# Leaving chunk steps out of table slots, and a block-diagonal product on quarters of the array

## The chip, the cores and the metric

The kernel runs on one NeuronCore of a Trainium2 chip. The metric is the time of one execution on the device, in microseconds (us); lower is better. All tensors are fp32.

## The reference, cut to what matters

The model has two layers. Layer 0 is a deformable attention block on `x` of shape (2, 512, 32, 32), followed by an output projection and an MLP with residuals; layer 1 is a plain attention over the 1024 positions with 512 channels. What matters here is the attention of layer 0:

```python
off = tanh(einsum(gelu(depthwise_6x6_stride4(q)), off_pw_w)) * 4      # per group: 64 key positions
kv  = grid_sample(xn, grid + off)                                      # (b, 512, 8, 8)
k   = gconv1x1(kv, kw);  v = gconv1x1(kv, vw)                          # 8 groups of 64 channels
pos  = grid_q[:, :, None, :] - grid_kv[:, None, :, :]                  # 1024 queries x 64 keys
bias = sign(pos) * log1p(abs(pos))
bias = relu(bias @ cpb_w1 + cpb_b1)                                    # 2 -> 128
bias = relu(bias @ cpb_w2 + cpb_b2)                                    # 128 -> 128
bias = bias @ cpb_w3 + cpb_b3                                          # 128 -> 1
attn = softmax(q k^T * scale + bias);  out = attn @ v
x    = x + einsum(out, out_w) + out_b
```

The bias network is evaluated for 16 (batch, group) pairs x 1024 queries x 64 keys, so its 128x128 layer is most of the arithmetic. The value weights `vw` are 8 separate 64x64 blocks; the kernel multiplies them into `out_w` once, so that the sampled features can be multiplied by the product directly.

## The kernel before

**Slots.** The bias network is worked through in 256 slots (`for s in range(NS)`), 16 for each pair of batch and group; a slot covers all queries for 4 keys. TensorE (PE) does 32 matmuls of layer 2 in a slot (`st_layer2`, L633): four groups `z`, each a PSUM tile of 128x1024 that four 32-column tiles of the array fill, in two instructions for each fp32 matmul. The profile therefore counts 64 records a slot. Before that, VectorE (DVE) writes layer 1's output `h1` (`st_layer1`, L616) two slots ahead of its use, in one of three buffers. After each group `z`, ScalarE (ACT) evicts it from PSUM with the ReLU (L642 into `rx`, L644 into `ua`, `uo`, `uc` or `ub`), and DVE sums pairs of evicted tiles (`st_sum`, L652). DMAs that add, issued by GpSimd (POOL) at L654 and L671 and by SyncE (SP) at L678 and L687, fold the sums further; `st_layer3` (L719, with the products of queries and keys at L702) takes the rest every eighth slot.

**PSUM.** The pool `zp` has three buffers of 128x1024. The four groups of a slot go through them in turn, and every other product in the slots (`flat(...)`) takes the next buffer of the same three.

**Table slots.** Each fourth slot (`s % 4 == 0`) also makes the layer-1 tables of the next four slots: a load on SP (`load_tables`, L585) and two ACT instructions (`st_tables`, L596 and L604), queued behind the eviction of group 1.

**Tails.** Softmax over finished logits (`softmax_steps`) is cut into steps too. A step runs in slots that are not table slots, behind the eviction of group 1 (in the last 16 slots in table slots too, there behind group 3). The exponentials (L757) of two pairs take eight steps, in slots 9, 10, 11, 13, 14, 15, 17 and 18 of each 32.

**Chunk steps.** What prepares the keys runs beside the slots, as a generator `bg = later()` of which one step is taken in a slot, behind the eviction of group 3:

```python
            st_sum(s, 0)
            if bg is not None:
                with tc.issue_after(evicted[s][1]):
                    next(bg, None)
```

`later()` first multiplies value weights and output weights (two steps, in slots 0 and 1, L503 and L507, into `uo`), then takes five chains of groups (`CHAINS`). A chain step computes queries (L267, L273, L279), the depthwise convolution (taps on ACT at L319, reductions on DVE at L334), Gelu (L343), the small product (L355), Tanh (L365), key positions (DVE L378 to L389), Abs and Ln on ACT (L392 to L396) and the correction on DVE (L398 to L405), whose result goes out by a DMA on SP to be read by `load_tables`. Its sampling steps (`sample`) prepare hat functions (L421 to L435, L449 to L458), multiply them on DVE (L463), gather with 16 small products (L471), scale and add (ACT L474, DVE L478), and multiply by key weights (L485) and by `uo` (L487), evicted at L491 and L493. They load their inputs on SP (L181, L184, L442, L444). In the profile the last chunk step's products stand in slot 154.

When all chains are through, the slot is noted as `ready`; 4 to 32 slots later DVE prepares blocks for the output projection in eight portions (`spread`, `fold`).

`wv` holds the value weights as four blocks of 128x128, each with two 64x64 blocks on its diagonal and zeros beside them. `QUADS` lists the four quarters of the array: `f_` is the half of the rows (contraction), `h_` the half of the output partitions.

Of the kernel before, what the change touches and what calls it, by code (L numbers as in the profile page):

```python
# [14 lines left out]
P = 128  # L15
B, C, H, W = 2, 512, 32, 32
HW = H * W
NCH = C // P
# [28 lines left out]
def conv_seq_kernel(ctx: ExitStack, tc: tile.TileContext, x, xt, kst, pst, cst, vec, wsm, outw, w1, w2, wl, wlt, brow, out):  # L47
    nc = tc.nc


    QUADS = [(slice(64 * f, 64 * f + 64), slice(64 * h, 64 * h + 64), f, h) for f in range(2) for h in range(2)]
# [50 lines left out]
    def fold(engine, w, sign=ALU.add, which=range(4)):  # L102
        for i in which:
            o, u, v = FOLD[i]
            engine.tensor_tensor(w[o], w[u], w[v], ALU.add if i % 2 else sign)
# [20 lines left out]
    def op_blocks(b, parts, wsum):  # L126
        v, q = vp[:, b * NCH : b * NCH + NCH, :], qa[:, b]
        w = [v[:, k : k + 2, n : n + 256] for k, n in ((0, 0), (2, 0), (2, 256), (0, 256))]
        x = [q[:, k : k + 2, n : n + 512] for k in (0, 2) for n in (0, 512)]
        return w + [wsum[:, j] for j in range(3)], x + [parts[:, j] for j in range(3)]  # L130
# [4 lines left out]
    def flat(name):  # L135
        return zp.tile([P, 2, 512], F32, tag="ps2", name=name).rearrange("p h n -> p (h n)")
# [4 lines left out]
    with tc.tile_pool(name="lp", bufs=2) as lp:  # L141
# [23 lines left out]
        wv = sx.rearrange("p a f j -> p (a f j)")[:, 0:512]  # L165
        ow_s = vp[:, 0:NCH, :]
# [26 lines left out]
        uo = vp[:, NCH : 2 * NCH, :]  # L193
# [302 lines left out]

        def later():

            for k2 in range(2):
                ps = flat("psu")  # L500
                for k in range(2):
                    c = 2 * k2 + k
                    nc.tensor.matmul(  # L503
                        ps[:, 512 * k : 512 * k + 512], wv[:, c * P : (c + 1) * P], ow_s[:, c, :],
                        start=True, stop=True,
                    )
                nc.scalar.copy(uo[:, 2 * k2 : 2 * k2 + 2, :].rearrange("p k o -> p (k o)"), ps)  # L507
                yield
            yield from sample(0)
            for ci in range(1, len(CHAINS)):  # L510
                yield from chain(ci)
                yield from sample(ci)
# [67 lines left out]
        def load_tables(c):  # L580
            b, k, f = groups[c // 4]
            ci, kk = chain_of[b, k]
            assert ci in state
            fb = lp.tile([P, 2, W, KT], F32, name="fb", bufs=1)
            nc.sync.dma_start(  # L585
                out=fb.rearrange("p a x j -> p (a x j)"),
                in_=fdr[ci][f * len(CHAINS[ci]) + kk, c % 4].rearrange("p j -> (p j)").partition_broadcast(P),
            )
            raw[c] = fb
# [18 lines left out]
        def st_layer1(s):  # L608
            ta, tb = tabs[4 * s // KT]
            j = 4 * s % KT  # L610
            h1 = lp.tile([P, H, 4, W], F32, name="h1", bufs=3)
            a = ta[:, j : j + 4, :].rearrange("p t x -> p (t x)")
            b = tb[:, j // 4].rearrange("p y t -> p (y t)")
            step = H // 2 if s == 0 else H
            for y in range(0, H, step):
                nc.vector._custom_dve(  # L616
                    TENSOR_ADD_SAT,
                    out=h1[:, y : y + step].rearrange("p y t x -> p (y t x)"),
                    in0=a.unsqueeze(1).to_broadcast([P, step, 4 * W]),
                    in1=b[:, 4 * y : 4 * (y + step)].unsqueeze(2).to_broadcast([P, 4 * step, W]),  # L620
                    s0=FMAX, s1=0.0,
                )
            h1s[s] = h1


        def st_layer2(s):
            h1 = h1s.pop(s)
            r = []
            for z in range(4):
                ps = zp.tile([P, 2, 512], F32, name="ps2")  # L630
                for h in range(2):
                    for q in range(4):
                        nc.tensor.matmul(  # L633
                            ps[32 * q : 32 * q + 32, h, :], cw2[:, 32 * z : 32 * z + 32],
                            h1[:, 16 * h : 16 * h + 16, q, :], start=True, stop=True,
                        )
                name, bufs = (
                    ("rx", 3), (("ua", 4), ("uo", 2), ("uc", 2), ("uo", 2))[s % 4], ("rx", 3), ("ub", 3)
                )[z]
                o = lp.tile([P, 2, 512], F32, name=name, bufs=bufs)  # L640
                if z % 2 == 0:
                    nc.scalar.activation(o, ps, AF.Relu, bias=sc[:, 4 + z : 5 + z])  # L642
                else:
                    nc.scalar.activation(o, ps, AF.Relu, bias=sc[:, 4 + z : 5 + z], scale=sc[:, z : z + 1])  # L644
                r.append(o)
                if z % 2 == 1:
                    evicted.setdefault(s, []).append(nc.cur_bb.bb.instructions[-1])
            sums[s] = r

        def st_sum(s, z):  # L650
            r = [t.rearrange("p h n -> p (h n)") for t in sums[s][z : z + 2]]
            nc.vector.scalar_tensor_tensor(r[1], r[0], sc[:, z : z + 1], r[1], ALU.mult, ALU.add)  # L652
            if z == 2 and s < NS - 1:
                nc.gpsimd.dma_start(out=sums[s][1], in_=sums[s][3], accum_op=ALU.add)  # L654
                added[0] = nc.cur_bb.bb.instructions[-1]
# [18 lines left out]
        def st_fold(s):  # L674
            add(lanes(s, 0), lanes(s, 1))

        def st_join(s):
            nc.sync.dma_start(out=lanes(s, 1), in_=lanes(s + 1, 1))  # L678
            add(lanes(s, 1), lanes(s + 1, 0))

        def st_fold2(s):
            for o, i in zip(twos(s, 0), twos(s, 1)):
                add(o, i)

        def st_join2(s):
            for o, i in zip(twos(s, 1), twos(s + 2, 1)):
                nc.sync.dma_start(out=o, in_=i)  # L687
            for o, i in zip(twos(s, 1), twos(s + 2, 0)):
                add(o, i)
# [91 lines left out]

        tails = []
        bg = later()
        load_tables(0)
        st_tables(0)
        st_layer1(0)
        st_layer1(1)
        for s in range(NS):
            if s > 0:
                st_sum(s - 1, 2)  # L790
            if s % 2 == 0 and 2 <= s < NS - 2:
                st_fold(s - 2)
            if s % 2 == 1 and 3 <= s < NS - 1:
                st_join(s - 3)
            if s % 4 == 0 and s >= 4:
                st_fold2(s - 4)
            if s % 4 == 2 and s >= 6:
                st_join2(s - 6)
            if s % 4 == 0 and s // 4 + 1 < 4 * NG:
                load_tables(s // 4 + 1)  # L800
            if s + 2 < NS:
                st_layer1(s + 2)
            st_layer2(s)


            if s % 4 == 0 and s // 4 + 1 < 4 * NG:
                with tc.issue_after(evicted[s][0]):
                    st_tables(s // 4 + 1)
            st_sum(s, 0)
            if bg is not None:  # L810
                with tc.issue_after(evicted[s][1]):
                    next(bg, None)
            if bg is not None and state.get(len(CHAINS) - 1, 0) is None:

                bg = None
                php.__exit__(None, None, None)
                opp = tc.tile_pool(name="op", bufs=1, side="right")
                op = opp.__enter__()
                op0 = op_blocks(
                    0, op.tile([P, 3, 2, 512], F32, name="op0x"), op.tile([P, 3, 2, 256], F32, name="op0w")  # L820
                )
                opt = op.tile([P, 2, 512], F32, name="opt")
                ready = s
            if bg is None and s > ready and (s - ready) % 4 == 0 and (s - ready) // 4 <= 8:
                i = (s - ready) // 4 - 1
                if i < 4:
                    spread(op0[1], (i,))
                else:
                    fold(nc.vector, op0[0], which=(i - 4,))
            if tails and (s % 4 or s >= NS - NSL):  # L830
                with tc.issue_after(evicted[s][s % 4 == 0]):
                    if next(tails[0], 0) is not None:
                        tails.pop(0)
            if s % 8 == 4 and s >= 12:
                st_layer3(s - 12)
                if s % NSL == 4:
                    tails.append(softmax_steps(s // NSL - 1))
# [37 lines left out]
    with ExitStack() as top, tc.tile_pool(name="wp", bufs=2) as wp:  # L875
# [171 lines left out]
        for i, (b, p) in enumerate(units):  # L1047

            j, k = divmod(i, NCH)
# [323 lines left out]
```

## Time and profile before

| | |
|---|---|
| median of 3 runs | 2662.8 us (2661.68 to 2663.64) |
| the profiled execution's own time | 2661.0 us |
| its span | 2659.2 us |
| granted TensorE clock | 1.00 |
| PE busy | 2633.2 us (99%) |
| DVE busy | 2241.3 us (84%) |
| ACT busy | 1687.2 us (63%) |
| slots, from 37.2 us on | 1867.3 us for 256 |

A page of the profile gives the busy time of each engine; matmuls overlap, so a busy PE can still hide gaps. A group is named by line, engine, operation and tiles (out<-in), with count, busy time, mean duration in ns of one, and the idle time of its engine just before it with what ended that (the releaser). A timeline line has start, duration, engine, line, operation and, in brackets, the idle time before it. PEld is the load of weights into the array, a row of its own. A window's line has its stretch and length, then each engine's busy time with the number of its instructions, the granted clock, the share of the DMA engines and GB/s.

### The profile page before, as it was taken

The page shows a single profiled execution, that of the slowest core. Times are in us where ns is not written, and L with a number is a line of the kernel's source. Part 1 is how long each engine was busy: PE and PEld are TensorE (multiplying, and loading weights), DVE is VectorE, ACT ScalarE, POOL GpSimd, SP SyncE. Part 2 cuts the span into 40 slices and gives each one's busy share as a digit, 9 for nine tenths or more (in the row PEclk, how much of TensorE's full clock was granted, in tenths as well). Part 3 has the DMA queues.
Part 4 walks back from the last instruction along what each step waited for, and adds up shares of the span by engine and source line. Part 5 has one row for each costly group of instructions (what it writes and reads, how often), then busy time and mean ns, then how long its engine had stood idle before and what let it go on. Part 6 is the DMA issues. An engine that isn't in the chain of part 4 may idle for free.

```text
span 2659.2 us, 46896 instructions
## 1 busy us (share of the span) xinstructions
PE 2633.2 (99%) x19344; PEld 965.0 (36%) x19344; DVE 2241.3 (84%) x1329; ACT 1687.2 (63%) x2201; POOL 792.3 (30%) x867
## 2 busy tenths in 40 slices
PE   9999999999999999999999999999999999999999
PEld 3332322433333333233323323333334444446454
DVE  7999999999999999999999999999674483466354
ACT  5887898789978888877777777777621131114041
POOL 1333333333333333333333333333343232000000
PEclk9999999999999999999999999999999999999999
DMA  5887878888788887888888888878730111000000
GB/s 187 181 176 169 191 164 171 181 189 180 171 176 174 192 175 172 171 177 176 171 172 183 175 178 178 172 173 181 191 110 33 48 48 48 0 16 0 32 0 32
DMA packets 116293, 366.77 MB, mean 138 GB/s; under 512 B 23376, under 2 KB 27616, under 8 KB 113392
## 3 DMA queue, kind: packets, MB, share of 16 engines
q0 software_dynamic: 69408, 235.31, 46.9%
q1 hardware_dynamic: 46240, 128.15, 13.8%
q8 instruction: 153, 2.51, 0.4%
q14 instruction: 60, 0.49, 0.1%
q10 hardware_dynamic: 432, 0.31, 0.0%
HBM read 74.81 MB, written 6.55 MB: 31 GB/s over the span
## 4 chain that ended last, share of the span: by engine, by line
PE 60%; DMA 25%; DVE 7%; issue 6%; ACT 1%; POOL 1%; SPq 0%; POOLq 0%; DVEq 0%; ACTq 0%
PE ps L633 31%; PE sw L956 14%; PE sw L1087 9%; DMA uc<-uo 7%; DMA uc<-uc 6%; DMA ua<-uc 4%; DMA uc<-ub 4%; DVE h L616 3%; PE sw L1185 2%; DMA ua<-uo 1%; DVE ub L652 1%; PE psg L535 1%; DMA ua<-ua 1%; PE sim L719 1%; DVE uo L652 1%
## 5 line engine op out<-in xcount | busy, mean ns | idle before, releaser
L633 PE MATMUL ps<-h,cw 128*32 128x512 f32 x16384 | 1782.8, 592 | 8.1 <-ACT rx L642 6.1
L616 DVE CUSTOM_DVE_ANT_1 h<-ta,tb 128x4096 f32<-128x4096 f32 (+1 forms) x257 | 1131.0, 4402 | 28.1 <-PE ps L633 24.2
L633 PEld LDWEIGHTS ps<-h,cw 128*32 128x32 f32 x16384 | 554.7, 110 | 1205.0 <-issue 1114.6
L642 ACT ACTIVATE rx<-ps,sc 128x1024 f32<-128x1024 f32 x512 | 568.1, 1110 | 146.3 <-PE ps L633 116.4
L644 ACT ACTIVATE ub<-ps,sc 128x1024 f32<-128x1024 f32 x256 | 308.2, 1204 | 80.5 <-PE ps L633 80.2
L652 DVE SCALAR_TENSOR_TENSOR ub<-rx,sc,ub 128x1024 f32<-128x1024 f32 x256 | 326.8, 1277 | 6.6 <-ACT ub L644 6.6
L671 POOL DMA_DIRECT2D ua<-uc x126 | 158.3, 1272 | 299.5 <-DMA ua<-uc 292.5
L671 POOL DMA_DIRECT2D ua<-ua x189 | 225.4, 1336 | 20.2 <-DMA ua<-uo 16.2
L644 ACT ACTIVATE uo<-ps,sc 128x1024 f32<-128x1024 f32 x128 | 154.2, 1205 | 74.3 <-PE ps L633 46.2
L956 PE MATMUL sw<-xb,w1t 128*128 128x512 f32 x448 | 193.7, 592 | 2.7 <-DVE xs L123 2.7
L956 PE MATMUL sw<-hm,w2t 128*128 128x512 f32 x448 | 193.6, 592 | 0.0
L654 POOL DMA_DIRECT2D uo<-ub x127 | 126.8, 998 | 210.8 <-DVE ub L652 200.1
L652 DVE SCALAR_TENSOR_TENSOR uo<-rx,sc,uo 128x1024 f32<-128x1024 f32 x128 | 163.5, 1278 | 18.9 <-ACT uo L644 18.9
L123 DVE TENSOR_TENSOR hm<-hm,sw 128x1024 f32<-128x1024 f32 x56 | 67.6, 1218 | 104.5 <-PE sw L956 104.3
L671 POOL DMA_DIRECT2D uc<-uo x63 | 54.0, 857 | 340.8 <-DMA uc<-uo 340.4
L956 PEld LDWEIGHTS sw<-xb,w1t 128*128 128x128 f32 x448 | 85.0, 190 | 110.2 <-issue 105.7
L965 ACT ACTIVATE hm<-hm,vs 128x512 f32<-128x512 f32 x64 | 42.6, 713 | 128.4 <-DVE hm L123 128.4
L956 PEld LDWEIGHTS sw<-hm,w2t 128*128 128x128 f32 x448 | 85.1, 190 | 107.1 <-issue 106.2
L123 DVE TENSOR_TENSOR xs<-xs,sw 128x1024 f32<-128x1024 f32 (+1 forms) x48 | 55.6, 1171 | 75.9 <-PE sw L1087 36.0
L654 POOL DMA_DIRECT2D ua<-ub x64 | 59.3, 926 | 178.4 <-DVE ub L652 163.4
L1087 PE MATMUL sw<-aT,vt 128*128 128x512 f32 x224 | 96.7, 593 | 0.3 <-ACT aT L1167 0.3
L596 ACT ACTIVATE ta<-fb,vs 128x512 f32<-128x512 f32 (+1 forms) x65 | 88.5, 1364 | 10.1 <-DMA fb<-fdr 10.1
(247 smaller groups left out, 2191.6 us busy)
## 6 DMA issues: line engine op xcount, KB each, us to landing
uo<-ub POOLq DMA_DIRECT2D x127, 512.0 KB, 5.5
fb<-fdr SPq DMA_DIRECT2D x64, 512.0 KB, 5.2
ua<-ub POOLq DMA_DIRECT2D x64, 512.0 KB, 6.0
uc<-ub POOLq DMA_DIRECT2D x64, 512.0 KB, 5.0
ua<-ua POOLq DMA_DIRECT2D x63, 256.0 KB, 6.3
ua<-uo SPq DMA_DIRECT2D x63, 256.0 KB, 2.5
ua<-uo POOLq DMA_DIRECT2D x63, 256.0 KB, 5.6
uc<-uc POOLq DMA_DIRECT2D x63, 256.0 KB, 7.2
```

What stands on the lines that cost most here:

```text
L123: nc.vector.tensor_tensor(out, a, b_, op)
L596: nc.scalar.activation(ta.rearrange("p j x -> p x j")[:, :, j0:j1], fb[:, 0, :, j0:j1], AF.Identity, bias=col("cb1"), scale=col("w1x"),)
L616: nc.vector._custom_dve(TENSOR_ADD_SAT, out=h1[:, y : y + step].rearrange("p y t x -> p (y t x)"), in0=a.unsqueeze(1).to_broadcast([P, ste ...
L633: nc.tensor.matmul(ps[32 * q : 32 * q + 32, h, :], cw2[:, 32 * z : 32 * z + 32], h1[:, 16 * h : 16 * h + 16, q, :], start=True, stop=True,)
L642: nc.scalar.activation(o, ps, AF.Relu, bias=sc[:, 4 + z : 5 + z])
L644: nc.scalar.activation(o, ps, AF.Relu, bias=sc[:, 4 + z : 5 + z], scale=sc[:, z : z + 1])
L652: nc.vector.scalar_tensor_tensor(r[1], r[0], sc[:, z : z + 1], r[1], ALU.mult, ALU.add)
L654: nc.gpsimd.dma_start(out=sums[s][1], in_=sums[s][3], accum_op=ALU.add)
L671: nc.gpsimd.dma_start(out=out, in_=in_, accum_op=ALU.add)
L956: nc.tensor.matmul(ps[:, m, :], w[:, a, k, m * P : (m + 1) * P], x[:, b_, k, :], start=(k == 0), stop=(k == 1),)
L1087: nc.tensor.matmul(ps[:, m, :], w[:, a, k, c + m * P : c + (m + 1) * P], x[b_][:, k, :], start=(k == 0), stop=(k == nk - 1),)
L1185: nc.tensor.matmul(v[:, m, :], xbl[b_][:, k, m * P : (m + 1) * P], gn[:, a, k, :], start=(k == 0), stop=(k == 1),)
```

## The change

Two edits. In the main loop, the chunk step is left out in table slots (`s % 4 == 0`) from slot 60 on, so that from there three steps are taken in four slots. In `later`, the four 128x128 products of value and output weights become, for each of the four, products on the four quarters of the array with only the diagonal 64x64 blocks as weights: half of the rows, half of the output partitions and 256 of the 512 columns each. Each of the four takes a PSUM buffer of its own, and its result is evicted in four copies of 64x256. Two of the four are still done in a step.

```diff
         def later():
 
-            for k2 in range(2):
+            for c in range(NCH):
                 ps = flat("psu")
-                for k in range(2):
-                    c = 2 * k2 + k
+                for f_, h_, f, h in QUADS:
                     nc.tensor.matmul(
-                        ps[:, 512 * k : 512 * k + 512], wv[:, c * P : (c + 1) * P], ow_s[:, c, :],
-                        start=True, stop=True,
-                    )
-                nc.scalar.copy(uo[:, 2 * k2 : 2 * k2 + 2, :].rearrange("p k o -> p (k o)"), ps)
-                yield
+                        ps[h_, f * 512 : f * 512 + 256], wv[f_, c * P + 64 * f : c * P + 64 * f + 64],
+                        ow_s[f_, c, h * 256 : (h + 1) * 256], start=True, stop=True,
+                    )
+                for f_, h_, f, h in QUADS:
+                    nc.scalar.copy(uo[f_, c, h * 256 : (h + 1) * 256], ps[h_, f * 512 : f * 512 + 256])
+                if c % 2 == 1:
+                    yield
             yield from sample(0)
...
             st_sum(s, 0)
-            if bg is not None:
+
+            if bg is not None and (s % 4 or s < 60):
                 with tc.issue_after(evicted[s][1]):
                     next(bg, None)
```

## The prediction

> **What bounds the kernel now.** I read the page first, then the busy time by stretch, then the idle time of TensorE (PE) by line, then the timeline at the few places where PE stood still. All of it is one execution: span 2659.2 us, own time 2661.0, so 1.8 us lie around the span. The median of the runs, 2662.8, is 1.8 above that execution; I add it at the end. Of this kernel a measurement can tell about 0.2%, 5.3 us, from no change.
>
> ```profile
> PE 2633.2 (99%) x19344; PEld 965.0 (36%) x19344; DVE 2241.3 (84%) x1329; ACT 1687.2 (63%) x2201; POOL 792.3 (30%) x867
> ```
>
> PE is the bound. The starts of the first matmul of each slot show it cleanly: a slot with nothing but its own matmuls lasts 6.867 us, so a gain must take PE work or PE idle time away. Where is PE idle? The busy time of each engine in four stretches: slots 0 to 59, slots 60 to 155 (the rest of the chunk steps), slots 156 to 187, slots 188 to 255.
>
> ```profile
> core 0: us, PE busy (x) PEld busy (x) DVE busy (x) ACT busy (x) POOL busy (x), PEclk, DMA share, GB/s
> 37.20:480.80 443.60, 439.16 (x4061) 134.02 (x4064) 430.82 (x231) 368.69 (x484) 149.26 (x171) 1.00 0.78 170
> 480.80:1193.50 712.70, 705.61 (x6629) 231.98 (x6625) 698.30 (x364) 605.50 (x841) 252.51 (x290) 1.00 0.82 179
> 1193.50:1420.10 226.60, 226.60 (x2106) 69.28 (x2102) 222.21 (x104) 171.27 (x196) 81.73 (x94) 1.00 0.81 174
> 1420.10:1904.50 484.40, 483.86 (x4482) 158.65 (x4476) 458.13 (x211) 363.27 (x428) 178.56 (x205) 1.00 0.82 175
> ```
>
> Length less PE busy: 4.4, 7.1, 0.0 and 0.5 us. PE is idle where chunk steps run and hardly anywhere else, and the new rule reaches only the 7.1 us of the second row: this one number caps the first edit. The groups of that stretch, PE alone, say what the idle time stands before (the last column):
>
> ```profile
> L633 PE MATMUL ps<-h,cw 128*32 128x512 f32 x6151 | 671.4, 593 | 3.4 <-ACT rx L642 3.4
> ...
> L485 PE MATMUL pkk<-kv,wk 128*128 128x64 f32 x12 | 2.6, 294 | 2.7 <-ACT rx L642 1.6 <-issue 1.1
> ```
>
> The remaining 1.0 is L471 (0.7) and L487 (0.3). Two causes. **A late eviction**, 4.4 us with L471 and L487: ScalarE (ACT) is in order, and when a chunk step on it waits, the next evictions come late. In slot 137 the Abs of L392 waited 2.29 us for VectorE's (DVE) L389, which stood behind a 4.42 us layer-1 instruction; the third eviction of the next slot was then late for PE:
>
> ```profile
> 1059.95 0.34 DVE L389 TENSOR_SCALAR fe<-th,cs 64x256 f32<-64x256 f32 x1
> ...
> 1060.32 0.42 ACT L392 ACTIVATE fe<-fe 64x256 f32<-64x256 f32 x1 [2.29 <-DVE fe L389]
> ...
> 1062.43 4.07 PE L633 MATMUL ps<-h,cw 128*32 128x512 f32 x36 [0.94 <-ACT rx L642]
> ```
>
> **A late sum**, 2.7 us: PE's key and value product L485 needs DVE's L478, which was in DVE's queue. The page's releaser says ACT, but the timeline shows L478 ending just before:
>
> ```profile
> 1138.13 0.20 DVE L478 TENSOR_TENSOR kv<-kv,uv 128x64 f32<-128x64 f32 x1
> ...
> 1138.40 0.30 PEld L485 LDWEIGHTS pkk<-kv,wk 128*128 128x128 f32 x2 [2.47 <-ACT rx L642]
> ```
>
> **What the Trainium skill says.** "ScalarE: Activation LUTs", What ACT_TABLE_LOAD costs: about 1283 ns for a load, more with the drain. The trace agrees: 1283 ns each, 5 before Gelu (L343), 5 before Exp (L757). "TensorEngine Tiling (Array Packing)", Key Properties: tiles of the array work independently, and a change of tiling mode drains TensorE. Agrees: one matmul start to the next is 0.43 us inside the slot's matmuls and 0.52 at a change, so 0.09 each. Same page, PSUM Bottleneck: tiling speeds up TensorE but not PSUM evacuation. This decides the second edit.
>
> **Second edit, the four products, in slots 0 and 1.** PE before: per step 4 records at 0.43 plus two changes of 0.09, 1.9 us (44.25 to 46.16, and 53.17 to 55.08). After: two chunks of 8 records each on quarters. The nearest row is the same shape in L487, where 8 records took 0.48 from start to the next line's start: 2 x 0.48 + 0.18 = 1.14. So 0.77 less a step, 1.5 in all, as a ceiling. But the step now takes two PSUM buffers of three, not one. The slot's last eviction frees the buffer that the next slot's first matmuls need, and those could begin only 0.11 after it:
>
> ```profile
> 44.85 1.20 ACT L644 ACTIVATE ub<-ps,sc 128x1024 f32<-128x1024 f32 x1
> ...
> 46.16 0.16 PEld L633 LDWEIGHTS ps<-h,cw 128*32 128x32 f32 x8 [0.76 <-ACT ub L644]
> ...
> 53.31 1.21 ACT L644 ACTIVATE ub<-ps,sc 128x1024 f32<-128x1024 f32 x1 [0.60 <-PE ps L633]
> ...
> 55.08 0.16 PEld L633 LDWEIGHTS ps<-h,cw 128*32 128x32 f32 x8 [0.76 <-ACT ub L644]
> ```
>
> In slot 0 that eviction ends at 46.05, so the next slot starts at 46.16 as before: gain 0 (its table work, 1.38 + 0.68 us on ACT, is what made it late). In slot 1 it ends at 54.52; start at 54.63 instead of 55.08: gain 0.45. ACT: two copies of 1.01 become sixteen of 0.367 (L493, the same 64x256 copy; four took 1.50), so a step has 3.0 us of copies. Slot 1's first eviction comes 0.85 later (49.0, not 48.16). Hidden: group two needs the first chunk's buffer, free at 47.5, and starts at 47.88; group three needs the second's, free at 49.0, and starts at 49.6. Without these 0.4 and 0.6 us of cover each late microsecond is one of PE. Bounds: a loss of 1.0 (both covers gone), a gain of 1.5. I take a gain of 0.45.
>
> **First edit.** Step k ran in slot k. From 60 on three steps take four slots: step 96 goes from slot 96 to 109, the last, 155, to 187. It adds no instruction; each step takes its ACT, DVE and PE instructions and its SP loads (L181, L442, L444) and store along, behind more table loads (L585) on SP. The keys of the last chain are wanted by table loads in slot 188 and its products in slot 212; steps 139 and 155 land in 166 and 187, so nobody waits. The blocks for the projection (`spread`, `fold`) move to slots 191 to 219, where DVE's layer 1 is some 9 us ahead of PE: hidden, and even 8 x 1.2 us in a row would be.
> ACT's load in a table slot: evictions 2 x 1.11 + 2 x 1.20 = 4.6, table 2.06, a three-tap step 3 x 0.53 = 1.6: 8.3 against 6.87. Without the step 6.7. But PE didn't pay for that overrun: over slots 78 to 81, one of them such a slot, length and PE busy are both 27.46. Three PSUM buffers carry it. So the gain is only at the stalls found above.
> Late sum, 2.7 us: DVE needs 4.35 + 2 x 1.19 = 6.73 us of a 6.867 slot, so its queue shrinks by 0.14 a slot, and by 0.9 to 1.1 in slots where PE does a layer-3 product or transposes. A chain's end puts 5.8 us on it within five steps (L378 to L405), and the first L478 comes nine steps later. Nine steps are now twelve slots: 3 x 0.14 and one extra slot of 1.0, about 1.4 us less queue against waits of 1.1 and 1.6. I leave 0.6 of 2.7: gain 2.1.
> Late eviction, 4.4 us: the chain's end meets the exponentials (slots 9 to 18 of each 32). That stays: before it was the last chain (steps 137 to 146), now it is the one before (steps 96 to 101 in slots 109 to 115), while the last chain's samples meet the exponentials at 169 to 178. Each burst is thinner by a quarter; I take a third of 4.4 away, 1.4. Bounds of this edit: a gain of all 7.1; a loss as in the third rival.
> Sum: 0.45 + 2.1 + 1.4 = 4.0. 2661.0 - 4.0 = 2657.0 for such an execution, 2658.8 as a median (-0.15%).
>
> **Rivals.**
> *All stalls go* (for it: slots 156 to 187, without chunk steps, have none; against: the chain's end still meets exponentials): 7.1 + 0.45 = 7.5, 2655.3.
> *Nothing moves but the products*: the stalls sit at ends of chains, whichever slots are left out; 2662.8 - 0.45 = 2662.3. For it: the overrun in table slots was free.
> *Slower, ACT between exponentials and chunk steps.* Steps meet three windows of exponentials from slot 60 on (24 steps); stretched, they meet four (32 steps, since both stay out of table slots). The idle time was 0.3 to 1.9 us a window, some 3.3 in these three. At 2.5 each, four cost 10: 6.7 more, less 0.45, 2669.0. It decides from 2.3 a window on; the dearest seen, slots 137 to 146, was 1.9.
>
> **How the numbers follow.** Likeliest case 0.58, with a range of its own from -1.5 to -7 (0.17 of it beyond 5.3); all stalls go 0.25; only the products 0.09; slower 0.08 (0.01 of it within the bound). Faster 0.17 + 0.25 = 0.42, same 0.41 + 0.09 + 0.01 = 0.51, slower 0.07. The range 2654 to 2664.5 leaves out the slower rival and the best end of the first.
>
> **What would show it.** Right: PE idle of slots 60 to 187 near 3.6 instead of 7.1; L485's idle under 1; slot 1 begins 8.94 after slot 0 as before, slot 2 some 8.5 after slot 1; L507's place holds sixteen copies. Wrong: idle above 7 in that stretch, idle before L633 in slots 169 to 178, or a late second slot behind the copies.

## The result, and the profile after

| | before | after |
|---|---|---|
| median of 14 runs each, side by side | 2661.72 us (2658.98 to 2665.62) | 2655.23 us (2653.69 to 2658.74) |
| the profiled execution's own time | 2660.99 us | 2656.55 us |
| its span | 2659.2 us | 2654.8 us |

The ratio after to before is 0.9975, 95% interval 0.9968 to 0.9982: 6.5 us less by the medians, 4.4 by the two profiled executions. The forecast was 2658.8 with a range of 2654 to 2664.5.

The engines' line of the page after:

```profile
PE 2633.2 (99%) x19368; PEld 977.5 (37%) x19368; DVE 2237.7 (84%) x1329; ACT 1689.5 (64%) x2215; POOL 791.2 (30%) x867
```

The page's totals tell almost nothing here: PE has the same busy time as before to a tenth. Fourteen more ACT instructions are the copies (2 became 16). The gain shows only where length and PE busy are set against each other. These are the same four stretches as before, cut at the slots' starts of this execution:

```profile
37.50:479.60 442.10, 437.70 (x4089) 135.58 (x4092) 430.66 (x231) 371.46 (x498) 148.88 (x171) 1.00 0.78 171
479.60:1185.40 705.80, 703.73 (x6584) 236.45 (x6580) 688.74 (x341) 591.31 (x797) 252.39 (x291) 1.00 0.83 180
1185.40:1414.20 228.80, 228.20 (x2154) 70.79 (x2150) 226.36 (x122) 184.82 (x241) 82.20 (x96) 1.00 0.81 175
1414.20:1898.60 484.40, 483.72 (x4482) 162.90 (x4476) 461.35 (x217) 363.47 (x429) 177.66 (x205) 1.00 0.82 175
```

Length less PE busy is now 4.4, 2.1, 0.6 and 0.7 us. In the second and third rows, which the rule reaches, it fell from 7.1 + 0.0 to 2.7. The work moved as told: the third row has 241 ACT instructions where it had 196, the second 797 where it had 841. What the rest of the idle time stands before, in the groups of PE over slots 60 to 187:

```profile
L634 PE MATMUL ps<-h,cw 128*32 128x512 f32 x8196 | 890.5, 592 | 2.5 <-ACT rx L643 2.1 <-ACT ub L645 0.3
...
L471 PE MATMUL pkv<-wt,xnt 128*64 128x64 f32 x192 | 6.9, 225 | 0.2 <-ACT uo L645 0.2
...
L487 PE MATMUL pkv<-vp,kv 64*64 64x256 f32 x48 | 4.0, 402 | 0.0
L485 PE MATMUL pkk<-kv,wk 128*128 128x64 f32 x12 | 2.6, 297 | 0.0
```

The late sum before L485 is gone, 2.7 to 0.0. The late evictions (L634, L471, L487) fell from 4.4 to 2.7. (L634 and L643 after are L633 and L642 before.)

The second edit, in the timeline of slots 0 and 1:

```profile
44.48 1.43 PE L502 MATMUL psu<-vp,sx 64*64 64x256 f32 x16
...
45.07 1.20 ACT L645 ACTIVATE ub<-ps,sc 128x1024 f32<-128x1024 f32 x1
...
46.16 3.03 ACT L507 COPY vp<-psu 64x256 f32<-64x256 f32 x8
46.33 0.16 PEld L634 LDWEIGHTS ps<-h,cw 128*32 128x32 f32 x8 [0.88 <-ACT ub L645]
...
53.33 1.09 PE L502 MATMUL psu<-vp,sx 64*64 64x256 f32 x16
...
53.47 1.21 ACT L645 ACTIVATE ub<-ps,sc 128x1024 f32<-128x1024 f32 x1 [0.60 <-PE ps L634]
...
54.73 0.16 PEld L634 LDWEIGHTS ps<-h,cw 128*32 128x32 f32 x8 [0.76 <-ACT ub L645]
```

In slot 1 the products are through at 54.42 (53.33 + 1.09), but the next slot's first weights load at 54.73, just after the eviction into `ub` ends (53.47 + 1.21 = 54.68). Slots 0 and 1 last 8.86 and 8.40 us instead of 8.94 and 8.92. The copies of step 0 run beside the next slot's matmuls, as foreseen, and slot 2 begins no later for them.

### The profile page after: what moved, and what is told of

Read it like the earlier page. It is cut to its first block, busy times and chain, and to the rows that moved or that the text cites. A ratio compares the mean times of both kernels' runs of the same rounds, so it can differ in the third digit from the quotient of the medians.

```text
span 2654.8 us, 46955 instructions
## 1 busy us (share of the span) xinstructions
PE 2633.2 (99%) x19368; PEld 977.5 (37%) x19368; DVE 2237.7 (84%) x1329; ACT 1689.5 (64%) x2215; POOL 791.2 (30%) x867
## 4 chain that ended last, share of the span: by engine, by line
PE 67%; DMA 14%; DVE 10%; issue 6%; ACT 2%; POOL 0%; DVEq 0%; SPq 0%; POOLq 0%; ACTq 0%
PE ps L634 37%; PE sw L958 15%; PE sw L1089 9%; DMA uc<-uo 5%; DVE h L617 5%; DMA uc<-uc 3%; DMA ua<-uc 2%; DVE ub L653 2%; PE sw L1187 2%; DMA ua<-uo 2%; DMA uc<-ub 1%; PE psg L536 1%; DVE uo L653 1%; PE sim L720 1%; PE sw L905 1%
## 5 line engine op out<-in xcount | busy, mean ns | idle before, releaser
L634 PE MATMUL ps<-h,cw 128*32 128x512 f32 x16384 | 1781.1, 592 | 7.5 <-ACT rx L643 5.3
L634 PEld LDWEIGHTS ps<-h,cw 128*32 128x32 f32 x16384 | 566.4, 110 | 1191.1 <-issue 1073.6
L643 ACT ACTIVATE rx<-ps,sc 128x1024 f32<-128x1024 f32 x512 | 567.3, 1108 | 144.2 <-PE ps L634 115.4
L992 ACT COPY hm<-sw 128x1024 f32<-128x1024 f32 x8 | 8.1, 1010 | 137.2 <-PE sw L958 137.2
```

Source lines behind the costliest of these rows:

```text
L634: nc.tensor.matmul(ps[32 * q : 32 * q + 32, h, :], cw2[:, 32 * z : 32 * z + 32], h1[:, 16 * h : 16 * h + 16, q, :], start=True, stop=True,)
```

## The experiments

The theory under test: thinning the chunk steps to three in four slots shortens what lies before the late sums and thins the clash with the exponentials, and it doesn't matter which slots are left out; the products bring what two PSUM buffers leave of them. The rivals: table slots are overfull on ACT, so that leaving out just these is what counts; or the products do it. The table gives the length of the slots in one profiled execution each, from the first matmul of one slot to that of another, and the runs' ratio to the kernel before on the same chip.

| kernel | slots 0, 1 | slots 60 to 187 | slots 0 to 254 | ratio, 95% |
|---|---|---|---|---|
| before | 8.94, 8.92 | 939.30 | 1860.37 | |
| after | 8.86, 8.40 | 935.04 | 1854.26 | 0.9975 (0.9968 to 0.9982) |
| rule alone | 8.92, 8.92 | 937.98 | 1856.02 | 0.9993 (0.9985 to 1.0001) |
| rule alone, again | 8.95, 8.92 | 938.40 | 1857.47 | 0.9988 (0.9980 to 0.9996) |
| products alone | 8.89, 8.40 | 941.74 | 1858.21 | 0.9990 (0.9983 to 0.9996) |
| products alone, again | 8.86, 8.40 | 939.66 | 1860.54 | 0.9997 (0.9989 to 1.0005) |
| other slots left out | 8.89, 8.40 | 936.77 | 1853.84 | 0.9971 (0.9959 to 0.9983) |
| exponentials' slots left out | 8.87, 8.40 | 934.54 | 1852.48 | 0.9973 (0.9962 to 0.9984) |
| spare step | 8.92, 8.92 | 940.33 | 1859.24 | 0.9999 (0.9991 to 1.0007) |
| sum on GpSimd | 8.92, 8.92 | 969.35 | 1897.78 | 1.0137 (1.0122 to 1.0153) |
| third `uo` | 8.85, 8.40 | 934.70 | 1855.45 | 0.9971 (0.9963 to 0.9979) |
| one buffer a step | 8.03, 8.03 | 935.03 | 1853.64 | 0.9972 (0.9962 to 0.9982) |
| one buffer, third `uo` | 8.03, 8.03 | 934.69 | 1852.16 | 0.9980 (0.9972 to 0.9987) |
| all four | 8.04, 8.03 | 960.97 | 1885.53 | 1.0104 (1.0090 to 1.0118) |

### Each edit alone, twice

The rule alone, on the kernel before:

```diff
-            if bg is not None:
+            if bg is not None and (s % 4 or s < 60):
```

> The rule alone: no chunk steps in table slots from slot 60 on, the products as before. Theory (thinning): from slot 60 on a slot carries less chunk work on ACT and DVE at the ends of chains, so evictions and the sums L478 come in time; nearly all of the change is this. PE idle of slots 60 to 187 is near the 2.7 us of the changed kernel (7.1 before), slots 0 and 1 as before (8.94 and 8.92), ratio to before 0.9976 to 0.9984. Rival (the products carry more than the 0.6 us seen in slots 0 and 1, by shifting what follows): ratio 0.999 or above.

The products alone, on the kernel after:

```diff
-            if bg is not None and (s % 4 or s < 60):
+            if bg is not None:
```

> The products on quarters alone, chunk steps in every slot. Theory (thinning): only the 0.6 us of slots 0 and 1 is gained; PE idle of slots 60 to 155 stays near 7.1 us, L485 still waits 2 us or more in all; ratio 0.9995 to 1.0000. Rival (products carry more): ratio 0.999 or below and the idle time from slot 60 on smaller.

By the medians the rule brought 1.7 us (2659.04 against 2660.74) and the products 2.7 (2658.04). That misses both expectations: nearly all of the change was to be the rule's, next to nothing the products', and both ratios lie where the rivals put them, though with the products alone the idle time did not fall (8.4 us). In slots 60 to 187 the rule alone took 7.1 - 4.1 = 3.0 us of idle time away, but only 1.3 us of length (939.30 to 937.98); the rest went into what the profile counts as busy PE. The groups of PE there, rule alone:

```profile
L633 PE MATMUL ps<-h,cw 128*32 128x512 f32 x8200 | 892.3, 592 | 4.1 <-ACT rx L642 2.1 <-ACT uo L644 1.6 <-ACT ub L644 0.4
...
L485 PE MATMUL pkk<-kv,wk 128*128 128x64 f32 x12 | 2.6, 299 | 0.0
```

And products alone:

```profile
L634 PE MATMUL ps<-h,cw 128*32 128x512 f32 x8192 | 893.9, 593 | 3.1 <-ACT rx L643 2.3 <-ACT uo L645 0.8
...
L487 PE MATMUL pkv<-vp,kv 64*64 64x256 f32 x48 | 4.0, 402 | 1.5 <-ACT rx L643 1.5
L485 PE MATMUL pkk<-kv,wk 128*128 128x64 f32 x12 | 2.5, 292 | 3.8 <-ACT ub L645 1.5 <-ACT rx L643 1.2 <-issue 1.0
```

The wait before L485 goes with the rule and stays without it: in three of its places in products alone (530, 833 and 1138 us) DVE's L478 ended 0.10 us before L485 began. The 0.5 us of slot 1 goes with the products. But the rule alone did not thin the late evictions: before L633, L471 and L487 they cost 4.4 us in the kernel before, 4.1 here and 2.7 after. Part of them are evictions into `uo`, which the prediction has no term for: 1.6 us here, 0.2 after. As the sum of the two was smaller than the whole, both kernels were run again on another chip:

> The rule alone again (as in the first experiment), beside the products alone on the same chip, since the two times of the first pair (0.9993 and 0.9990) add up to less than the changed kernel's 0.9975. Theory (the two effects add, the first pair was scatter): slots 60 to 187 last 935 to 938 us, ratio 0.9978 to 0.9990. Rival (the rule gains only together with the products): slots 60 to 187 at 939 us or more, ratio 0.9992 or above.

> The products alone again. Theory (they gain 0.6 us in slots 0 and 1 and nothing else): slots 60 to 187 last 939 to 942 us, slots 0 and 1 8.9 and 8.4; ratio 0.9990 to 1.0000, with the middle near 0.9995. Rival (the products change what follows as well): slots 2 to 59 or 60 to 187 shorter by 1 us or more than the kernel before's 425.7 and 939.3, and the ratio 0.9988 or below.

Slots 60 to 187 came out within 0.5 us of the first time for the rule alone, again with no idle time before L485, and within 2.1 for the products alone, with 3.3 there. The late evictions of the rule alone were again no fewer:

```profile
L633 PE MATMUL ps<-h,cw 128*32 128x512 f32 x8198 | 892.3, 592 | 4.6 <-ACT rx L642 3.3 <-ACT uo L644 0.7 <-ACT ub L644 0.4
```

The medians were 3.4 and 1.8 us under the kernel before (2658.22 and 2659.85 against 2661.64). The mean of both rounds is 2.6 for the rule and 2.2 for the products, 4.8 together, against 6.5 for both edits at once; each interval is about 2 us to either side, so the medians don't contradict a plain sum.

### Which slots are left out

On the kernel after, the other slots are those with `s % 4 == 2`:

```diff
-            if bg is not None and (s % 4 or s < 60):
+            if bg is not None and (s % 4 != 2 or s < 60):
```

> The changed kernel, but from slot 60 on the slots left out are s % 4 == 2 instead of the table slots (s % 4 == 0): the same thinning, three steps in four slots, while chunk steps meet the tables again. Theory (thinning): about as fast as the changed kernel, ratio to before 0.9975 to 0.9985, L485 idle under 0.7 us. Rival (table slots are what counts: tables plus step overrun ACT there by 1.4 us): the idle time of slots 60 to 187 stays at 6 us or more, ratio 0.9990 to 1.000.

And the eight slots of 32 in which exponentials run:

```diff
-            if bg is not None and (s % 4 or s < 60):
+            if bg is not None and (s % 4 == 0 or not 9 <= s % 32 <= 18 or s < 60):
```

> The changed kernel, but the slots left out from slot 60 on are those with exponentials (slots 9, 10, 11, 13, 14, 15, 17, 18 of each 32, 8 of 32 as table slots are); table slots take chunk steps again. Theory A (thinning alone counts): as the changed kernel, ratio 0.9975 to 0.9985. Theory B (the late evictions that are left come from steps that meet exponentials): late evictions before L634 from slot 60 on fall from 2.5 us to under 1, ratio 0.9970 or below. Rival (table slots are what counts): idle 6 us or more, ratio 0.9990 to 1.000.

Both are as fast as after: medians 2653.80 and 2653.50 where before had 2660.74, slots 60 to 187 936.8 and 934.5. With chunk steps in every table slot nothing is lost, so the rival of overfull table slots falls. With the quartered products and no step left out these slots last 941.7 and 939.7 us, so what counts here is the quarter fewer steps. The trace of a difference is before L485. With the other slots left out, where under 0.7 was expected:

```profile
L485 PE MATMUL pkk<-kv,wk 128*128 128x64 f32 x12 | 2.6, 297 | 0.8 <-ACT rx L643 0.8
```

With the exponentials' slots left out:

```profile
L634 PE MATMUL ps<-h,cw 128*32 128x512 f32 x8196 | 891.8, 592 | 1.7 <-ACT rx L643 1.4 <-ACT ub L645 0.3
...
L485 PE MATMUL pkk<-kv,wk 128*128 128x64 f32 x12 | 2.6, 297 | 1.0 <-issue 1.0
```

The 1.0 is a single late sum at 531 us, in slot 66: this rule leaves out nothing from slot 60 up to there, so that chain is as crowded as before. The 0.8 is the same sum, in slot 68. In the kernel after, table slot 68 is left out between the sum's step in slot 67 and the product's in slot 69, and the sum was there 7.2 us early. So for this one sum it does matter which slots are left out. The evictions' 1.7 are less than the 2.5 after, but the expectation for the clash at the exponentials was under 1, with a ratio of 0.9970 or below: in one execution it is not shown.

### The late sum by itself

Can the late sum be had without thinning? First by moving the addition off DVE, on the kernel before:

```diff
-                nc.vector.tensor_tensor(kv, kv, uv, ALU.add)
+                nc.gpsimd.tensor_tensor(kv, kv, uv, ALU.add)
```

> The kernel before with one edit: the sum L478 (scaled features plus the bias term, 128x64) runs on GpSimd instead of DVE, so that PE's L485 no longer waits for DVE's queue. Theory (late sums in DVE's queue are 2.7 us of the idle time from slot 60 on): idle before L485 falls from 2.7 us to under 0.5 in the profile, late evictions before L633 stay at 3 to 5 us; ratio 0.9985 to 0.9995. Rival (L485 was late for ACT's eviction, as the page's releaser says): idle before L485 stays at 2 us or more, ratio 0.9995 to 1.0005; if GpSimd's queue of adding DMAs holds the sum up instead, it grows.

A clear miss, 36 us slower (2698.53 against 2662.31). The waits of PE (us in total, times, longest) and the addition's own line (ns: shortest, median, longest):

```profile
PE pkk L485 <- POOL kv L478: 31.5, 4, 8.7
```

```profile
L478 POOL TENSOR_TENSOR kv<-kv,uv x8: 884/4218/10469, 107.4 to 1220.6; 128x64 f32<-128x64 f32 x8
```

DVE's same addition took 0.2 us. On GpSimd the eight took 0.9 to 10.5. A timeline shows what ran beside one of the long ones:

```profile
539.00 9.19 POOL L478 TENSOR_TENSOR kv<-kv,uv 128x64 f32<-128x64 f32 x1
540.01 1.27 DVE L652 SCALAR_TENSOR_TENSOR ub<-rx,sc,ub 128x1024 f32<-128x1024 f32 x1
541.21 1.27 DVE L652 SCALAR_TENSOR_TENSOR uc<-rx,sc,uc 128x1024 f32<-128x1024 f32 x1
542.40 4.41 DVE L616 CUSTOM_DVE_ANT_1 h<-ta,tb 128x4096 f32<-128x4096 f32 x1
546.74 1.27 DVE L652 SCALAR_TENSOR_TENSOR ub<-rx,sc,ub 128x1024 f32<-128x1024 f32 x1
...
548.24 0.69 PE L485 MATMUL pkk<-kv,wk 128*128 128x64 f32 x2 [8.71 <-POOL kv L478]
```

GpSimd's addition ended at 548.19, 0.18 after the last of DVE's unbroken run (546.74 + 1.27). The Trainium skill, "SBUF — State Buffer", Who interferes with whom, says that a DVE instruction with two SBUF inputs contends with a GpSimd one that reads SBUF, that the ports they share are an exclusive lock, and that issue order decides who blocks. DVE's L652 and L616 have two such inputs, and the 9.19 us fit that; no run here separates the port from other causes. The clock adds to the waits: behind them PE's matmuls ran at half of it (the 0.50 of this window):

```profile
543.40:553.60 10.20, 5.36 (x30) 1.77 (x34) 4.60 (x2) 1.69 (x5) 9.15 (x6) 0.50 0.46 96
```

Second, by an empty step in the last three chains, so that the sums fall in other slots, on the kernel before:

```diff
                 xn0.append(...)
                 yield
+                if ci >= 2:
+                    yield
```

> The kernel before with an empty chunk step between the sum L478 and the product L485 in the chains from the third on (six steps more, chunk steps in every slot): DVE has a slot more to get to L478. Theory (L485's wait of 2.7 us is DVE's queue, which a slot more covers): idle before L485 under 0.3 us; late evictions before L633, 3 to 5 us, stay, as chains still end within five slots; slots 60 to 187 last 936 to 938 us; ratio 0.9985 to 0.9995. Rival (time given to steps does not help, only fewer steps in a slot do): idle before L485 1.5 us or more, 939 us or more, ratio 0.9995 to 1.0005.

The groups of PE in slots 60 to 187 (here the key and value product is L487, the product with `uo` L489):

```profile
L635 PE MATMUL ps<-h,cw 128*32 128x512 f32 x8196 | 893.0, 592 | 7.1 <-ACT rx L644 4.8 <-ACT uo L646 1.8 <-ACT ub L646 0.4
...
L489 PE MATMUL pkv<-vp,kv 64*64 64x256 f32 x48 | 4.0, 402 | 0.4 <-ACT rx L644 0.3
L487 PE MATMUL pkk<-kv,wk 128*128 128x64 f32 x12 | 2.6, 299 | 0.0
```

The late sum went to zero, as expected, and the time did not move, where 0.9985 to 0.9995 was expected: 0.9999 (0.9991 to 1.0007). Late evictions stand in its place: 7.1 us before layer 2's groups where they had been 3.4, 1.8 of it at `uo`. So the late sum was DVE's queue, and to take it away by moving a step was worth nothing; whether the spare step itself made the evictions late is not shown by one execution.

### The two PSUM buffers of the products

On the kernel after, both products of a step go into one buffer, with four copies of 64x512 a step instead of eight of 64x256:

```diff
-                        ps[h_, f * 512 : f * 512 + 256], ...
+                        ps[h_, f * 512 + k * 256 : f * 512 + k * 256 + 256], ...
...
-                    nc.scalar.copy(uo[f_, c, h * 256 : (h + 1) * 256], ps[h_, f * 512 : f * 512 + 256])
+                    nc.scalar.copy(uo[f_, 2 * k2 : 2 * k2 + 2, h * 256 : (h + 1) * 256], ps[h_, f * 512 : (f + 1) * 512])
```

> The changed kernel, but the two products of a step share one PSUM buffer (half of the columns each) and are evicted together, four copies of 64x512 a step instead of eight of 64x256. Theory of the prediction (the second buffer makes the next slot's first group wait for the last eviction): slots 0 and 1 last 8.1 to 8.2 us each instead of 8.86 and 8.40, about 1.0 us less in all, and no wait for ub before the next slot; ratio 0.0003 below the changed kernel's. Rival (PE's own time for the quarters is what is left): 8.86 and 8.40 again.

The same place in the timeline as shown of after:

```profile
52.54 1.09 PE L505 MATMUL psu<-vp,sx 64*64 64x256 f32 x16
...
52.68 1.20 ACT L650 ACTIVATE ub<-ps,sc 128x1024 f32<-128x1024 f32 x1 [0.60 <-PE ps L639]
...
53.56 0.16 PEld L639 LDWEIGHTS ps<-h,cw 128*32 128x32 f32 x8 [0.39 <-issue]
```

The next slot begins at 53.56, while the eviction into `ub` runs until 53.88. PE waits for nobody, and slots 0 and 1 last 8.03 each. Against after that is 0.83 and 0.37 us, 1.2 in all: what the second buffer cost.

### A third buffer for `uo`

On the kernel after (the room in SBUF comes from letting two short-lived tiles share other tiles' buffers):

```diff
-                    ("rx", 3), (("ua", 4), ("uo", 2), ("uc", 2), ("uo", 2))[s % 4], ("rx", 3), ("ub", 3)
+                    ("rx", 3), (("ua", 4), ("uo", 3), ("uc", 2), ("uo", 3))[s % 4], ("rx", 3), ("ub", 3)
```

> The changed kernel with three buffers for the evicted tile uo instead of two (room is made by letting two small key tiles share memory with others). Theory: a part of the idle time, different from execution to execution, is the first group of a slot waiting for an eviction into uo that waited for an adding DMA out of the buffer (0.2 to 2 us in each profile so far); with three buffers no first group waits for uo, and the ratio to before is 0.0002 to 0.0007 below the changed kernel's (0.9968 to 0.9974). Rival (these waits are ACT's own lateness): such waits stay, ratio as the changed kernel's.

ACT's waits before its evictions into `uo`, before:

```profile
ACT uo L644 <- DMA ua<-uo: 11.8, 8, 2.1
ACT uo L644 <- DMA uc<-uo: 10.9, 8, 2.9
```

After:

```profile
ACT uo L645 <- DMA uc<-uo: 17.6, 11, 3.4
ACT uo L645 <- DMA ua<-uo: 15.5, 13, 1.9
```

And with the third buffer, where neither of these lines is left:

```profile
ACT uo L645 <- PE ps L634: 49.3, 86, 0.6
```

So by the releasers named, ACT stood 22.7 us before and 33.1 after, in the whole execution, for an adding DMA of GpSimd (L671 of the kernel before; the DMAs of SP at L678 and L687 copy) to finish reading `uo`. Of the 33.1, the third buffer took all away and PE got 0.3 back (935.0 to 934.7 in slots 60 to 187): three PSUM buffers carry a late eviction of a microsecond or two. They don't always. In products alone, one such wait ran through to PE:

```profile
876.24 1.21 ACT L645 ACTIVATE uo<-ps,sc 128x1024 f32<-128x1024 f32 x1 [2.79 <-DMA ua<-uo]
...
877.50 0.30 PEld L485 LDWEIGHTS pkk<-kv,wk 128*128 128x128 f32 x2 [0.99 <-ACT uo L645]
...
878.01 1.10 ACT L643 ACTIVATE rx<-ps,sc 128x1024 f32<-128x1024 f32 x1
...
879.15 0.66 PE L487 MATMUL pkv<-vp,kv 64*64 64x256 f32 x8 [1.22 <-ACT rx L643]
```

The eviction into `uo` came 2.79 late, the next one behind it at 878.01, and L487, which needs the buffer that this one frees, began 0.04 after its end with 1.22 us lost. L485's own sum was there in time (DVE's L478 ended at 875.57): this loss comes by way of ACT and PSUM, not by a late sum.

### All together

The exponentials' slots left out, the sum on GpSimd, the third `uo` and one buffer a step:

> The changed kernel with four edits together: slots with exponentials left out instead of table slots, L478 on GpSimd, three buffers for uo, one PSUM buffer a step for the products. Theory: the three causes of idle time in the slots (late sums, late evictions, waits for uo) are separate and each edit takes its own; slots 60 to 187 last 933 us or less (935.1 in the changed kernel, 939.3 before, 930 without any wait), ratio 0.9960 to 0.9968. Rival (the edits take the same waits twice, or GpSimd's queue brings new ones): 0.9970 or above.

2688.79 us, 26.5 more than before, where 0.9960 to 0.9968 was expected: the sum on GpSimd, with 28.3 us of waits before L485, outweighs the rest. Without it, and with the kernel's own rule, the two buffer edits:

> The changed kernel with three buffers for uo and one PSUM buffer a step for the products, the two edits that helped apart. Theory (they take different waits): slots 0 and 1 last 8.03 each, no first group of a slot waits for uo, slots 60 to 187 last 935 us or less; ratio to the kernel before 0.9962 to 0.9972, below the changed kernel's 0.9975. Rival (what is won in the slots is within the scatter of what is lost elsewhere): ratio 0.9973 to 0.9980.

The slots 0 to 254 were the shortest of all kernels with the table rule, 1852.16 us, 2.1 less than after; its median, 2656.14 against 2661.64 for before, is no better than after's. The profiled execution lost it outside the slots: the first slot began at 39.29 instead of 37.47, and 766.2 us followed the start of slot 255 instead of 763.1. None of the versions that have both edits and the sum on DVE can be told from after.

## Why the prediction was right, point by point

The direction and the place held, and of the three terms the late sums and the products are shown with their causes. The term for the late evictions came out in size, but thinning alone does not bring it. The gain was larger than the forecast. Of the slots' 6.1 us (1860.37 to 1854.26), slots 60 to 187 gave 4.3 and slots 0 and 1 0.6; the other 1.2 lie elsewhere, 0.9 of it in slots 28 to 40, before the rule begins (99.48 to 98.62; the two executions of the rule alone, which run the same code there, gave 97.47 and 99.16). The start (+0.25) and the work after the slots (+1.4) took some of it back, which leaves the 4.4 of the spans. That this lies so near the forecast's 4.0 is luck: it is a larger gain in the slots less a loss outside them, and in slots 60 to 187 the rule alone, for which 3.5 was forecast, brought 1.3 and 0.9.

- **Late sums**: forecast 2.1 of 2.7, measured 2.7 of 2.7. The rule alone does it (0.0 twice), and it stays where the rule leaves a chain unthinned (1.0 in slot 66). DVE's queue can be read as the time from the end of L474, whose result the sum takes, to the start of L478. Before, in front of the sum of the last chain that started at 1138.13, and after, at the same step of that chain:

```profile
1129.93 0.31 ACT L474 ACTIVATE kv<-pkv,bns 128x64 f32<-128x64 f32 x1
```

```profile
1337.78 0.30 ACT L474 ACTIVATE kv<-pkv,bns 128x64 f32<-128x64 f32 x1
...
1344.34 0.21 DVE L478 TENSOR_TENSOR kv<-kv,uv 128x64 f32<-128x64 f32 x1
...
1344.62 0.30 PEld L485 LDWEIGHTS pkk<-kv,wk 128*128 128x128 f32 x2 [0.84 <-ACT rx L643]
```

  That is 7.9 us before (L485 in slot 148) and 6.3 after (slot 178), and 7.4 and 6.0 at the other late sum (slots 107 and 123). The queue is 1.6 and 1.4 us shorter, as worked out (1.4), which just covers the waits of 1.6 and 1.1: in slot 178 the sum ended 0.1 us before L485 began. In the two executions of the rule alone it was 2.2 to 3.9 us shorter. The 0.6 that the forecast kept back was not needed.
- **Late evictions**: forecast 1.4 of 4.4, measured 1.7. A third taken for a burst thinned by a quarter was a choice, and that the size fits is luck as far as the runs show. With the rule alone 4.1 and 4.6 us were left, with the products alone 4.6 and 5.3; only both together bring them down, to 2.7 after and 1.4 to 3.7 in the other versions with the sum on DVE. The prediction also named only the exponentials. Part of the late evictions are those into `uo`, held by DMAs: 0.7 of the 4.4 before (the wait before L471), 1.6 and 0.7 in two executions of the rule alone, 0.2 after and 0.0 with a third `uo`.
- **Products**: forecast 0.45, measured 0.60. The reason, the second PSUM buffer, is shown by the one-buffer version. Slot 1 came out at 8.40 (forecast some 8.5), and slot 0 gained 0.08 where 0 was forecast. By the medians the products alone brought 2.2; where the rest of it would lie is not shown. The forecast's ceiling of 1.5 for the products without that wait was low: one buffer gives 8.94 + 8.92 - 8.03 - 8.03 = 1.8.
- **The copies**, costed at nothing with cover of 0.4 and 0.6 us: slots 2 to 27 took 186.56 us before and after. Right.
- **The rivals**: *all stalls go* was wrong in mechanism, as 2.7 us of idle remain, although its 2655.3 is the time that came out. *Only the products* falls with the products alone (0.9990 and 0.9997 against 0.9975) and with the rule alone, which takes the wait before L485 away. *Slower, ACT between exponentials and chunk steps* fell: all four windows together stayed under the 2.7 us, where it needed more than 2.3 each.
- **The base**: the forecast added 1.8 us from the profiled execution to a median. Over 14 runs the kernel before lay 0.7 above its profiled execution, and after lay 1.3 below its own. Here a term was mis-sized: of the 3.6 us between forecast and median, 1.1 come from this (2662.8 became 2661.7) and the rest from the gain, 6.5 instead of 4.0.
- **Chances**: a gain over 0.2% was given 0.42 and no measurable change 0.51. The measured 0.25% lies just over that edge, so the likeliest case, right in direction and place, fell by its size on the other side.

**What stays open.** Slots 60 to 187 lasted 940.2 us on average over the three executions with a step in every slot (before, products alone twice) and 938.2 with the rule alone, but 934.7 to 935.0 in all four with the table rule and quartered products. These four are 3.3 us shorter than the rule alone, though the products have long been done by slot 60. The difference sits in late evictions: PE's idle time before layer 2 is 4.1 and 4.6 us with the rule alone and 1.4 to 2.5 in the four. From slot 3 on, ACT, DVE, POOL and SP run the same instructions in the same order with and without the products. A shift of the three PSUM buffers against the slots, as the products take four turns instead of two, is not the reason: with one buffer a step they take two turns as before, and those versions stand at 935.0 and 934.7 too. One place can be named. In both executions of the rule alone PE lost 1.16 us in slot 112, behind an eviction into `uo` in slot 111 before which ACT stood idle for 2.0 and 1.7 us. It began within 0.1 us of the landing of an adding DMA out of `uo`, 6.2 and 5.8 us into that slot; after, that DMA landed 2.9 us into it, with one buffer 3.9, and ACT did not wait. Why it landed later with the rule alone was not found.

## What to carry to other kernels

Where one engine is busy 99% of the time, set length against its busy time stretch by stretch, and put a price only on the idle time that the change can reach: that number (7.1 us here) bounded the first edit, and of it 4.4 came. Spreading a background task thinner took one kind of stall away by itself, the late sums, and the late evictions only together with the other edit; moving a step in the schedule ended the same late sums and gained no time. So run each of two edits alone before giving either its term of a sum. And a product that takes one more buffer of a rotating set can pay for it with a wait for the oldest one: two products in the halves of one buffer were 1.2 us better than in two buffers.

## What the hardware showed that was not expected

- **Half clock after short waits.** In products alone, after the waits at 877 to 880 us shown above, PE's matmuls ran at half speed for 3.4 us. Two windows of that execution:

```profile
873.00:889.50 16.50, 15.19 (x124) 4.23 (x120) 12.16 (x9) 9.97 (x21) 4.09 (x6) 0.90 0.87 213
880.00:884.50 4.50, 4.50 (x26) 1.00 (x28) 4.29 (x2) 1.88 (x7) 0.00 (x0) 0.62 1.07 225
```

  The third number from the end is the clock, 0.62 over 4.5 us. That is 3.4 us at 0.5 and the rest at 1.0, and costs 1.7 us. The Trainium skill, "TensorE: Matmul & The Clock Gate", What's actually happening, has a clock halved after an idle window of some 3.4 us. The length agrees, the condition does not: no single wait was over 1.22 us here, and some 2 us of the 3.4 before the fall at 880.5 were work (0.3 until 877.4, then 0.43 in L485, 0.66 in L487 and 0.9 from 879.6 on). So such a wait can cost more than its own length.
- **It can decide between two profiles.** The profiled execution of after has such a stretch after its slots, behind a wait of 3.86 us, and that of before has none there:

```profile
1961.00:1964.50 3.50, 3.50 (x6) 1.46 (x5) 0.00 (x0) 0.00 (x0) 1.47 (x2) 0.52 0.98 377
```

  Its cost of 1.7 us is of the size of the 1.4 that the work after the slots took back of the slots' 6.1; other differences there were not counted.
- **A small sum on GpSimd** beside a DVE that hardly rests took 0.9 to 10.5 us, against 0.2 on DVE. Its waits of up to 8.7 us cost clock as well: slots 60 to 187 lasted 30 us longer than before, 23.2 of it idle time of PE and 6.8 busy time, and three stretches of 6.8 to 10.2 us at half clock lie in them.
